# A four-layer network in one kernel: transposes widened to 128 columns, an MLP begun on one step's statistics, and a Fourier layer whose row 64 and last unit are rescheduled

## The chip, the cores and the metric

The kernel runs on one core of one Trainium2 chip, as one program. The metric is device time in microseconds (us), the median of three runs. The engines: PE multiplies matrices (PEld loads its weights), DVE works on vectors, ACT applies functions and copies, POOL is a second vector engine, SP issues the DMAs. On-chip memory is SBUF; matmuls write PSUM[...].

## The reference, cut to what matters

The input is x[4, 96, 64, 64]; with b = 4 images of L = 4096 tokens there are NT = 16384 tokens of C = 96 channels. Layer 0 (two Mamba blocks) and layer 2 (linear attention, a quantised MLP) are not touched by the change. Layer 1 and the first half of layer 3 are:

```python
# layer 1: depthwise 7x7 convolution, LayerNorm over channels, MLP with gelu, residual
h = conv7x7_depthwise(x, conv_w) + conv_b
h = transpose(h, (0, 2, 3, 1))
h = (h - mean(h)) * rsqrt(var(h) + eps) * ln_g + ln_b
h = gelu(einsum('bhwc,cf->bhwf', h, w1) + b1)          # 96 -> 384
x = transpose(einsum('bhwf,fc->bhwc', h, w2) + b2) * layer_scale + x
...
# layer 3, first half: Fourier mixing along the 4096 tokens, on t = LayerNorm(t)
h = relu(bn(einsum('bnc,hc->bnh', t, w1)))             # 96 -> 192
X = fft(h, axis=1)
xr = relu(X.real * rd - X.imag * idg + rb)
xi = relu(X.imag * rd + X.real * idg + ib)
y = ifft(xr + 1j * xi, axis=1).real
t = t + bn(einsum('bnh,ch->bnc', y, w2))
```

## The kernel before, in words

The residual stream `t` stays in SBUF as [96, 16384]. The layers follow each other; in the profiled execution layer 1 lies at about 2605 to 3011 us, the Fourier layer at 3300 to 3838 us, and the last quantised MLP behind it.

**Layer 1, turn.** `tokens` (L730) loads one of 16 chunks of 1024 tokens: layer 0's output `o` and the input `xr`, 393 KB each; ACT scales `o` and DVE adds the two (L737). `turn` (L739) brings the chunk to tokens on partitions: for each 128 tokens one matmul (L744) with the tokens as the weights (96 rows, 128 columns) and an identity of 96 columns as the moving operand. Four results share a PSUM tile; ACT copies the first four, DVE the second four (L748) into `xt`. A matmul on 32-bit data is two passes through PE, so a chunk has 16 passes. The next chunk's `tokens` is written ahead of each `turn`. Then the convolution follows as 24 groups of four channels, each four matmuls with 128x128 bands (L787, L790). `small` (L772) lends a slot of the same PSUM tag to `consts2`, which prepares weights of later layers at group 8.

**Layer 1, MLP.** The tokens come in 32 blocks of 512, in n = 8 steps k of four. `stats(k, d)` (L804) takes mean and variance of four rows of 128 tokens (bn_stats and bn_aggr on DVE); `roots(k)` (L813) makes rsqrt of a step's 16 variances on ACT, with Ln (L815) and Exp (L816), each behind a load of its table; `back(i)` (L818) normalises block i on DVE (L824), turns it back by four matmuls (L829) and copies it to `xc`; `hidden(i)` (L833) has three matmuls (L838) with gelu on ACT (L839); `out(i)` (L841) three matmuls (L844) and the addition to `t`. The order of each engine's instructions is written out by hand (L850 to L871): stats and roots of steps 0 and 1, then back(0) to back(3), then the steps. In step k, `hidden` of block 4k + d is followed by `back` of the block four ahead, stats of step k + 2, and `out` of the block before; roots(k + 2) ends the step.

**Fourier layer.** A transform over 4096 tokens is split into 128 x 32. There are eight units (image, half of the 192 hidden channels), and each unit has PER = 4 groups, so 32 groups `its`. The loop (from L1251) runs over j and is a software pipeline, again in an order written by hand. Iteration j has `over_n1(j)` (first transform, L1139), `fold(j-2)`, `over_n2(j-1)` (second, L1160 to L1163), and `over_k2(j-3)` (inverse over k2, L1208 and L1209, written to `bt`). Groups of unit u finish over_k2 in iteration 4u + 6. The real transform needs only 65 of 128 rows; row 64 takes a way of its own: `row64(u)` (L1215) multiplies (L1218), ACT copies to `r` (L1220), one DMA writes `r` to DRAM (`d<-r`, L1222) and a second one reads it back into row 64 of `bt` (`bt<-d`, L1223). It stands in iteration 4u + 7, behind over_k2. From iteration 4u + 8 on, unit u's eight blocks of four n follow, two in each iteration: `over_k1` (L1225) loads 256 KB of the inverse transform (`gt`), has four matmuls (L1230) into a `misc` bank, and ACT copies the result to `ys` (L1232); `w2` (L1234) multiplies it with the output weights (L1238) into another `misc` bank and DVE adds it to `t` (L1242 for half 0, L1244 for half 1). The order within an iteration with blocks is

```python
over_n1(j) ... fold(j - 2); over_k1(block 0); over_n2(j - 1) ...
w2(block 0); over_k1(block 1); over_k2(j - 3) ... row64; w2(block 1)
```

`misc` (L1098) has two PSUM banks, shared by six uses; tag `i1` of over_k2 has two as well. Iterations also carry work for the next image: LayerNorm (`norm1`, `norm2`) where unit j // 4 is even, `w1` ("tokens") where it is odd, and nothing for the last unit. Past j = 31 only the pipeline's rest is left; the last unit's blocks are iterations 36 to 39.

Of the kernel before, what the change touches and what calls it, by code (L numbers as in the profile page):

```python
# [9 lines left out]
F32 = mybir.dt.float32  # L10
# [8 lines left out]
B, C, HW, L = 4, 96, 64, 4096  # L19
# [31 lines left out]
class Net:  # L51
# [661 lines left out]
    def layer1(self, scratch, t):  # L713
# [4 lines left out]
        with ExitStack() as ctx:  # L718
# [4 lines left out]
            with (  # L723
                tc.manual_schedule(engines=engines),
                tc.tile_pool(name="l1a", bufs=1) as wk,
                tc.tile_pool(name="l1ap", bufs=1, space=PSUM) as psum,
            ):
                for at in (slice(0, 2), slice(NR + 2, NR + 4)):
                    nc.gpsimd.memset(xt[:, :, :, at], 0.0)
                def tokens(b, s):  # L730
                    at = slice(b * L + s * T, b * L + (s + 1) * T)
                    o = wk.tile([C, T], F32, name="o", tag="o", bufs=3)
                    nc.sync.dma_start(o, scratch[:, at])
                    xr = wk.tile([C, T], F32, name="xr", tag="xr", bufs=3)
                    nc.sync.dma_start(xr, ins["x"][b, :, s * T : (s + 1) * T])
                    nc.scalar.activation(o, o, AF.Identity, scale=self.osc, bias=self.osh)
                    nc.vector.tensor_add(t[:, at], o, xr)  # L737

                def turn(b, s):  # L739
                    for h in range(2):  # L740
                        ps = psum.tile([128, 4, C], F32, name="xt_ps", tag="xt", bufs=4)
                        for d in range(4):
                            a = b * L + s * T + (4 * h + d) * 128
                            nc.tensor.matmul(ps[:, d], t[:, a : a + 128], self.ident[:C, :C], start=True, stop=True)  # L744
                        r = 2 + s * (T // 128) + 4 * h
                        dst = xt[:, :, b, r : r + 4].rearrange("p c r -> p r c")
                        if h:
                            nc.vector.tensor_copy(dst, ps)  # L748
                        else:
                            nc.scalar.copy(dst, ps)  # L750

                chunks = [(b, s) for b in range(B) for s in range(NSC)]
                tokens(*chunks[0])
                for k, chunk in enumerate(chunks):
                    if k + 1 < len(chunks):
                        tokens(*chunks[k + 1])
                    turn(*chunk)

                def load(g):
                    w = wk.tile([128, GC, 4, 128], F32, name="band", tag="band", bufs=3)  # L760
                    nc.sync.dma_start(w, ins["band"][g])
                    return w

                def outer(g):

                    x2 = wk.tile([128, 2 * GC, B, NR], F32, name="x2", tag="x2", bufs=3)
                    at = slice(g * 2 * GC, (g + 1) * 2 * GC)
                    nc.gpsimd.tensor_copy(x2[:64], xt[:64, at, :, 4:])
                    nc.gpsimd.tensor_copy(x2[64:], xt[64:, at, :, :NR])
                    return x2  # L770

                def small(rows, cols):  # L772
                    ps = psum.tile([128, 4, C], F32, name="w_ps", tag="xt", bufs=4)
                    return ps.rearrange("p a c -> p (a c)")[:rows, :cols]

                x2 = [outer(0)]
                for g in range(C // GC):
                    if g == 8:
                        self.consts2(wk, small)
                    if g % 2 == 0 and g + 2 < C // GC:  # L780
                        x2.append(outer(g // 2 + 1))
                    w = load(g)
                    ps = psum.tile([128, GC, B, NR], F32, name="cv_ps", tag="cv", bufs=4)
                    for d in range(GC):
                        c = g * GC + d
                        for k, j in enumerate((1, 0, 2)):
                            nc.tensor.matmul(  # L787
                                ps[:, d], w[:, d, j], xt[:, c, :, 1 + j : 1 + j + NR], start=k == 0, stop=False
                            )
                        nc.tensor.matmul(ps[:, d], w[:, d, 3], x2[g // 2][:, g % 2 * GC + d], start=False, stop=True)  # L790
                    for d in range(GC):
                        c = g * GC + d
                        dst = xt[:, c, :, 2 : 2 + NR]
                        if g % 2:
                            nc.vector.tensor_scalar_add(dst, ps[:, d], cb[:, c : c + 1])
                        else:
                            nc.scalar.activation(dst, ps[:, d], AF.Identity, bias=cb[:, c : c + 1])
# [52 lines left out]
            n = NT // MB // 4  # L850
            with tc.manual_schedule(engines=engines):
                nc.scalar.preload_act_table_set(ACT_EXP_LN)
                for k in range(2):
                    for d in range(4):
                        stats(k, d)
                    roots(k)
                for d in range(4):
                    back(d)
                for k in range(n):
                    for d in range(4):  # L860
                        hidden(4 * k + d)
                        if k + 1 < n:
                            back(4 * k + 4 + d)
                        if k + 2 < n:
                            stats(k + 2, d)
                        if d:
                            out(4 * k + d - 1)
                    if k + 2 < n:
                        nc.scalar.preload_act_table_set(ACT_EXP_LN)
                        roots(k + 2)  # L870
                    out(4 * k + 3)  # L871
# [212 lines left out]
    def fourier(self, dram, t, h):  # L1084
        tc, nc, ins = self.tc, self.nc, self.ins
        CG, G, K1 = 24, 6, 65
        PER = CG // G
        units = [(b, half) for b in range(B) for half in range(2)]
        its = [(u, g) for u in range(len(units)) for g in range(0, CG, G)]
        with ExitStack() as ctx:  # L1090
# [7 lines left out]
            def misc(rows):  # L1098
                return pln.tile([128, MB], F32, name="m_ps", tag="m", bufs=2)[:rows]
# [98 lines left out]
            def over_k2(i):  # L1198

                u, g = its[i]  # L1200
                z = zz.pop(i)
                if g == 0:
                    bt[u] = wk.tile([N1, N2, C], F32, name="bt", tag="bt", bufs=2)
                for e in range(0, G, 3):
                    ps = pln.tile([N1, 3, 128], F32, name="i1_ps", tag="i1", bufs=2)
                    for d in range(3):
                        zd = z[:, e + d].rearrange("p k m -> p (k m)")
                        nc.tensor.matmul(ps[:, d], zd[:, 64:], bc, start=True, stop=False)  # L1208
                        nc.tensor.matmul(ps[:, d], zd[:, :128], bs, start=False, stop=True)  # L1209
                    nc.scalar.copy(  # L1210
                        bt[u].rearrange("p n (g c) -> p g n c", c=4)[:, g + e : g + e + 3],
                        ps.rearrange("p g (n c) -> p g n c", c=4),
                    )

            def row64(u):  # L1215
# [6 lines left out]
                nc.sync.dma_start(d.rearrange("o (n g c) -> g (o n) c", n=N2, c=4), r)  # L1222
                nc.sync.dma_start(bt[u][64:65].rearrange("p n c -> p (n c)"), d)  # L1223

            def over_k1(u, n, kept):  # L1225
                gt = wk.tile([N1, 4, N1], F32, name="gt", tag="gt", bufs=2)
                nc.sync.dma_start(gt, ins["idft"][:, n : n + 4])
                ps = misc(C).rearrange("p (n a) -> p n a", n=4)
                for d in range(4):
                    nc.tensor.matmul(ps[:, d], bt[u][:, n + d], gt[:, d], start=True, stop=True)  # L1230
                kept[u, n] = wk.tile([C, MB], F32, name="ys", tag="ys", bufs=2)
                nc.scalar.copy(kept[u, n], ps.rearrange("p n a -> p (n a)"))  # L1232

            def w2(u, n, kept):  # L1234

                b, half = units[u]
                ps = misc(C)
                nc.tensor.matmul(ps, self.a_w2[:, half, :], kept.pop((u, n)), start=True, stop=True)  # L1238
                ps = ps.rearrange("p (n a) -> p n a", n=4)
                td = ft[b][:, n : n + 4]  # L1240
# [6 lines left out]
            with tc.manual_schedule(engines=engines):  # L1247
                for n in range(0, N2, 2):
                    w1(0, n)
                kept, sq = {}, {}  # L1250
                for j in range(len(its) + 12):  # L1251
                    ub, k = divmod(j - 2 * PER, PER)
                    blocks = [(ub, n) for n in (8 * k, 8 * k + 4)] if 0 <= ub < len(units) else []

# [9 lines left out]

                    if j < len(its):
                        over_n1(j)

                    if normed:
                        norm1(b, a, sq)
# [18 lines left out]
                        over_k2(j - 3)  # L1288
                    if normed:
                        norm2(a, sq)  # L1290
                    if (j - 7) % PER == 0 and 0 <= (j - 7) // PER < len(units):
                        row64((j - 7) // PER)
                    turn(len(tokens))
                    if blocks:
                        w2(*blocks[1], kept)
                    if normed and k == PER - 1:
                        norm2(a + MB, sq)


def build(tc, ins, out):  # L1300
# [155 lines left out]
```

## Time and profile before

| | |
|---|---|
| runs | 3976.82, 3974.91, 3973.95 us; median 3974.91 |
| profiled execution | 3972.29 us; span in the trace 3970.5 us |
| mean granted PE clock | 0.858 of full |
| PE, DVE, ACT, POOL busy | 3291.6 (83%), 3155.9 (79%), 2419.9 (61%), 2912.9 (73%) us |
| gt<-in_idft | 64 DMAs of 256 KB |
| Fourier layer's iterations, start to start (L1139) | 11.6 to 15.4 us mostly; j = 12: 22.00, j = 20: 21.82, j = 28: 15.58 |

The busy share is an average over layers of which each has its own limit, so it says nothing of these stages. How to read what follows: a table by stretch of time gives each engine's busy time, the granted PE clock and the DMA share; the timeline lists instructions in order, with the idle time before them and its releaser in brackets; the waits list who waited for whom, with the sum, the number and the longest.

### The profile page before, as it was taken

To read this page: it belongs to the slowest core of one execution; us is meant where nothing else is said; L and a number is where in the kernel's file an instruction comes from. 1 tells how busy PE (TensorE), PEld (TensorE's weight loads), DVE (VectorE), ACT (ScalarE), POOL (GpSimd) and SP (SyncE) were. 2 spreads that over 40 slices of the span, in tenths; PEclk is the share of its full clock that TensorE was granted. 3 is DMA by queue.
4 is the path that set the end of the run, shared out by engine and by line. 5 is a ranking of instruction groups with operands and counts; after the bars stand their busy time and mean duration, and the time that the engine had idled before them with its cause. 6 is when DMAs were issued, how large, how long until landed. Compare 5 with 4: busy or idle time off the path is not lost. (4 is left out here: it accounts for less than half of the span.)

```text
span 3970.5 us, 45322 instructions
## 1 busy us (share of the span) xinstructions
PE 3291.6 (83%) x14174; PEld 1420.1 (36%) x14174; DVE 3155.9 (79%) x2772; ACT 2419.9 (61%) x4644; POOL 2912.9 (73%) x1443
## 2 busy tenths in 40 slices
PE   7888788888888778888878888677899998999878
PEld 3222222222222222222222222167445535666643
DVE  5999999999999999999999999941662384444539
ACT  4676667666666766677666666431345586655548
POOL 2999999999999999999999999911001064534417
PEclk8888888888887888788888888658899999999989
DMA  7567656756675667566666766566000000011111
GB/s 185 135 161 174 144 148 159 175 142 159 160 173 132 164 166 170 132 167 166 159 147 158 170 148 154 120 170 227 11 0 1 1 1 6 22 33 33 43 44 58
DMA packets 183291, 468.12 MB, mean 118 GB/s; under 512 B 53237, under 2 KB 55167, under 8 KB 179969
## 3 DMA queue, kind: packets, MB, share of 16 engines
q1 hardware_dynamic: 183048, 465.21, 47.1%
q8 instruction: 113, 1.85, 0.2%
q14 instruction: 130, 1.06, 0.1%
HBM read 391.53 MB, written 73.50 MB: 117 GB/s over the span
## 5 line engine op out<-in xcount | busy, mean ns | idle before, releaser
L496 POOL TENSOR_TENSOR hs<-hs,crep 128x1024 f32<-128x1024 f32 x768 | 1796.6, 2364 | 27.3 <-DVE hs L490 23.7
L454 PE MATMUL rep<-dbl,sel_b 32*128 32x512 f32 x1152 | 406.1, 781 | 464.1 <-DVE hs L490 433.4
L474 POOL TENSOR_TENSOR up<-udb,brep 128x1024 f32<-128x1024 f32 x256 | 605.1, 2364 | 8.5 <-DMA brep<-cd 8.5
L468 ACT ACTIVATE da<-ddb,nega 128x1024 f32<-128x1024 f32 x512 | 585.0, 1150 | 16.2 <-DVE hs L490 8.2
L468 ACT ACTIVATE dap<-ddb,nega 128x1024 f32<-128x1024 f32 x256 | 286.2, 1118 | 423.7 <-DVE hs L490 421.9
L515 PE MATMUL y<-hs,sel_r 128*32 128x512 f32 x3072 | 483.3, 689 | 6.5 <-POOL hs L496 6.4
L490 DVE TENSOR_TENSOR_SCAN hs<-da,state,rep 128x1024 f32<-128x1024 f32 x192 | 450.8, 2348 | 16.7
L490 DVE TENSOR_TENSOR_SCAN hs<-da,state,u 128x1024 f32<-128x1024 f32 x192 | 450.9, 2348 | 11.2 <-DVE u L486 1.4
L490 DVE TENSOR_TENSOR_SCAN hs<-dap,state,up 128x1024 f32<-128x1024 f32 x192 | 447.0, 2328 | 6.8 <-ACT dap L468 6.8
L454 PEld LDWEIGHTS rep<-dbl,sel_b 32*128 32x128 f32 x1152 | 109.0, 218 | 760.9 <-issue 512.8
L210 PE MATMUL ps<-n,w_x 97*64 97x512 f32 x1536 | 364.8, 617 | 9.4 <-ACT n L323 5.3
L486 DVE TENSOR_TENSOR u<-udb,rep 128x1024 f32<-128x1024 f32 x256 | 314.6, 1229 | 42.5 <-PE rep L454 11.3
L486 DVE TENSOR_TENSOR rep<-udb,rep 128x1024 f32<-128x1024 f32 x256 | 310.6, 1213 | 0.4
L1039 POOL CAST hq<-y 128x1536 fp8e5<-128x1536 f16 x64 | 93.9, 1467 | 253.7 <-issue 144.0
L210 PEld LDWEIGHTS ps<-n,w_x 97*64 97x64 f32 x1536 | 108.9, 140 | 257.5 <-issue 210.9
L515 PEld LDWEIGHTS y<-hs,sel_r 128*32 128x32 f32 x3072 | 66.9, 116 | 363.5 <-issue 195.8
L382 POOL TENSOR_TENSOR du<-delta,xc 128x512 f32<-128x512 f32 x96 | 122.6, 1277 | 67.4 <-ACT delta L366 52.2
L1178 POOL TENSOR_TENSOR av<-av,ec 128x780 f32<-128x780 f32 x32 | 58.8, 1837 | 150.1 <-ACT av L1175 150.1
L224 PE MATMUL ps<-xc,xproj 64*102 64x512 f32 x384 | 160.3, 998 | 3.5 <-ACT xc L344 3.5
L358 ACT COPY dbl<-ps 102x512 f32<-102x512 f32 x64 | 34.4, 589 | 207.1 <-PE ps L224 207.1
L911 POOL MEMSET h<- 1x4096 f32 x1 | 3.5, 3506 | 213.1 <-DVE n L824 213.1
L490 DVE TENSOR_TENSOR_SCAN hs<-da,rep 128x1024 f32<-128x1024 f32 x64 | 146.5, 2289 | 5.4
(256 smaller groups left out, 6492.9 us busy)
## 6 DMA issues: line engine op xcount, KB each, us to landing
ddb<-dd SPq DMA_DIRECT2D x768, 128.0 KB
udb<-ud SPq DMA_DIRECT2D x768, 128.0 KB
crep<-cd SPq DMA_DIRECT2D x512, 128.0 KB
brep<-cd SPq DMA_DIRECT2D x256, 128.0 KB
dd<-delta SPq DMA_DIRECT2D x64, 384.0 KB
ud<-du SPq DMA_DIRECT2D x192, 128.0 KB
band<-in_band SPq DMA_DIRECT2D x24, 1024.0 KB
gt<-in_idft SPq DMA_DIRECT2D x64, 256.0 KB
```

Of the source, the lines that this page charges most:

```text
L210: nc.tensor.matmul(ps[rows], w[:, 64 * p : 64 * p + 64], rhs[:, at.start + shift : at.stop + shift], start=k == 0, stop=k == len(ws) - 1, ...
L224: nc.tensor.matmul(ps, w[rows, p], x[rows, p], start=start and p == 0, stop=p == 2)
L382: nc.gpsimd.tensor_mul(u, m["delta"][:, of], m["xc"][:, of])
L454: nc.tensor.matmul(x[:, at], sel_b[rows, order[t][1]], made[k]["dbl"][rows, at], start=True, stop=True)
L468: nc.scalar.activation(da, made[k]["dd", h, j], AF.Exp, scale=nega[:, col : col + 1])
L474: nc.gpsimd.tensor_mul(u, made[k]["ud", h, j], made[k]["brep", g])
L486: nc.vector.tensor_mul(u, made[k]["ud", h, j], x)
L490: nc.vector.tensor_tensor_scan(hs[:, 1:], made[k].pop(("da", t)), u, 0.0 if s == 0 else st, ALU.mult, ALU.add)
L496: nc.gpsimd.tensor_mul(hs[:, :T], hs[:, 1:], made[k]["crep", order[t][1]])
L515: nc.tensor.matmul(made[k]["y", p][row : row + 32], sel_r, made[k]["hs", t][:, at], start=False, stop=True, skip_group_check=True,)
L1039: nc.gpsimd.tensor_copy(q, y2, saturate=False)
L1178: nc.gpsimd.tensor_add(v[:, 2:4], v[:, 0:2], ec)
```

## The change

In the turn, the matmul's moving operand has 128 columns (the identity's 96 rows, all its columns), and the PSUM tile is widened to 4 x 128[...]; the copies read the first 96 columns. In the MLP, only stats(0), roots(0) and back(0) stand ahead of the first hidden; back runs two blocks ahead instead of four; step 0 carries the stats of steps 1 and 2, and roots(1) stands behind hidden(2). In the Fourier layer row64(u) moves from iteration 4u + 7 to 4u + 6. The last unit's blocks leave the loop: all eight follow behind it, each over_k1 ahead of the w2 of the block before, and these w2 use the two `i1` banks. From j = 25 on, two loads of 1 MB into a free `hh` buffer take the place of the last 26 of the 256-KB loads.

```diff
-    ps = psum.tile([128, 4, C], F32, name="xt_ps", tag="xt", bufs=4)
+    ps = psum.tile([128, 4, 128], F32, name="xt_ps", tag="xt", bufs=4)
...
-    nc.tensor.matmul(ps[:, d], t[:, a : a + 128], self.ident[:C, :C], start=True, stop=True)
+    nc.tensor.matmul(ps[:, d], t[:, a : a + 128], self.ident[:C], start=True, stop=True)
...
-    nc.vector.tensor_copy(dst, ps)
+    nc.vector.tensor_copy(dst, ps[:, :, :C])
...
     nc.scalar.preload_act_table_set(ACT_EXP_LN)
-    for k in range(2):
-        for d in range(4):
-            stats(k, d)
-        roots(k)
     for d in range(4):
-        back(d)
+        stats(0, d)
+    roots(0)
+    back(0)
     for k in range(n):
         for d in range(4):
-            hidden(4 * k + d)
-            if k + 1 < n:
-                back(4 * k + 4 + d)
-            if k + 2 < n:
+            i = 4 * k + d
+            hidden(i)
+            if k == 0 and d == 2:
+                nc.scalar.preload_act_table_set(ACT_EXP_LN)
+                roots(1)
+            for i2 in (1, 2) if i == 0 else (i + 2,):
+                if i2 < 4 * n:
+                    back(i2)
+            if k == 0:
+                for d2 in (2 * (d % 2), 2 * (d % 2) + 1):
+                    stats(1 + d // 2, d2)
+            elif k + 2 < n:
                 stats(k + 2, d)
             if d:
-                out(4 * k + d - 1)
+                out(i - 1)
...
+    def fetch(k):
+        g = wk.tile([N1, CG, N2, 4], F32, name="hh", tag="hh", bufs=3)
+        g = g.rearrange("p g n c -> p (g n c)")[:, : N2 // 2 * N1].rearrange("p (n a) -> p n a", n=N2 // 2)
+        nc.sync.dma_start(g, ins["idft"][:, k * N2 // 2 : (k + 1) * N2 // 2])
+        for n in range(0, N2 // 2, 4):
+            late[k * N2 // 2 + n] = g[:, n : n + 4]
...
     def over_k1(u, n, kept):
-        gt = wk.tile([N1, 4, N1], F32, name="gt", tag="gt", bufs=2)
-        nc.sync.dma_start(gt, ins["idft"][:, n : n + 4])
+        if n in late:
+            gt = late[n]
+        else:
+            gt = wk.tile([N1, 4, N1], F32, name="gt", tag="gt", bufs=2)
+            nc.sync.dma_start(gt, ins["idft"][:, n : n + 4])
...
     def w2(u, n, kept):
-        ps = misc(C)
+        if u < len(units) - 1:
+            ps = misc(C)
+        else:
+            ps = pln.tile([N1, 4, 128], F32, name="i1_ps", tag="i1", bufs=2)[:C].rearrange("p n a -> p (n a)")
...
-    for j in range(len(its) + 12):
+    for j in range(len(its) + 4):
...
+        if j in (len(its) - 7, len(its) - 3):
+            fetch((j - len(its) + 7) // 4)
...
-        if (j - 7) % PER == 0 and 0 <= (j - 7) // PER < len(units):
-            row64((j - 7) // PER)
+        if (j - 6) % PER == 0 and 0 <= (j - 6) // PER < len(units):
+            row64((j - 6) // PER)
...
+    last = [(len(units) - 1, n) for n in range(0, N2, 4)]
+    for k, block in enumerate(last):
+        over_k1(*block, kept)
+        if k:
+            w2(*last[k - 1], kept)
+    w2(*last[-1], kept)
```

More of the change, by code (lines that the diff above doesn't have):

```diff
@@ L747, in turn @@
                         if h:
-                            nc.vector.tensor_copy(dst, ps)
+                            nc.vector.tensor_copy(dst, ps[:, :, :C])
                         else:
-                            nc.scalar.copy(dst, ps)
+                            nc.scalar.copy(dst, ps[:, :, :C])
                 chunks = [(b, s) for b in range(B) for s in range(NSC)]
@@ L772, in small @@
                 def small(rows, cols):
-                    ps = psum.tile([128, 4, C], F32, name="w_ps", tag="xt", bufs=4)
+                    ps = psum.tile([128, 4, 128], F32, name="w_ps", tag="xt", bufs=4)
                     return ps.rearrange("p a c -> p (a c)")[:rows, :cols]
@@ L1204, in over_k2 @@
                 for e in range(0, G, 3):
-                    ps = pln.tile([N1, 3, 128], F32, name="i1_ps", tag="i1", bufs=2)
+                    ps = pln.tile([N1, 4, 128], F32, name="i1_ps", tag="i1", bufs=2)[:, :3]
                     for d in range(3):
@@ L1223, in row64 @@
                 nc.sync.dma_start(bt[u][64:65].rearrange("p n c -> p (n c)"), d)
-            def over_k1(u, n, kept):
-                gt = wk.tile([N1, 4, N1], F32, name="gt", tag="gt", bufs=2)
-                nc.sync.dma_start(gt, ins["idft"][:, n : n + 4])
+            late = {}
+            def fetch(k):
[4 more added lines that the diff above has]
+                    late[k * N2 // 2 + n] = g[:, n : n + 4]
+            def over_k1(u, n, kept):
+                if n in late:
[3 more added lines that the diff above has]
+                    nc.sync.dma_start(gt, ins["idft"][:, n : n + 4])
                 ps = misc(C).rearrange("p (n a) -> p n a", n=4)
```

## Prediction

> **What bounds the kernel now.** No engine alone: PE is busy 83% of the span, but the change touches four stretches, each with its own limit. I read first the busy time by stretch, because it gives the granted clock (PEclk) of each. Columns: stretch, length, busy time of PE, weight loads, DVE, ACT, POOL, clock, DMA share, GB/s.
>
> ```profile
> 2614.00:2669.00 55.00, 54.42 (x255) 54.42 (x256) 28.66 (x31) 28.91 (x31) 0.00 (x0) 0.50 0.95 262
> 2676.00:2690.00 14.00, 14.00 (x128) 14.00 (x127) 2.26 (x8) 2.29 (x8) 4.78 (x5) 1.00 0.76 253
> 2842.00:3011.00 169.00, 167.14 (x529) 79.73 (x527) 95.45 (x309) 74.48 (x105) 4.06 (x2) 1.00 0.00 1
> 3765.00:3838.00 73.00, 50.27 (x247) 34.38 (x246) 22.90 (x26) 19.98 (x42) 5.73 (x4) 0.84 0.18 51
> ```
>
> Row 1 is layer 1's turn: PE is never idle, at half clock. Row 2, the convolution's 128-column passes, runs at full clock: 14.00/128 = 0.109 us a pass, against 54.42/255 = 0.213 in the turn. Row 3, the MLP's steady part, is PE-bound at full clock, 24.66 us a step. Row 4 is the Fourier tail, PE busy 69%.
>
> Next the timeline, for the pace inside the turn (start, length, engine, line, in brackets idle time before and its releaser):
>
> ```profile
> 2616.35 1.22 DVE L737 TENSOR_TENSOR t<-o,xr 96x1024 f32<-96x1024 f32 x1 [1.83 <-DMA xr<-in_x]
> 2619.42 1.22 DVE L737 TENSOR_TENSOR t<-o,xr 96x1024 f32<-96x1024 f32 x1 [0.27 <-DMA xr<-in_x]
> 2629.24 1.20 DVE L737 TENSOR_TENSOR t<-o,xr 96x1024 f32<-96x1024 f32 x1
> 2632.66 1.20 DVE L737 TENSOR_TENSOR t<-o,xr 96x1024 f32<-96x1024 f32 x1
> ```
>
> The first chunks come every 3.07 us, as the loads land; later ones every 3.41, which is 16 passes of 0.213. PE sets the pace by only 0.34 us a chunk.
>
> The MLP's start, PE and ACT:
>
> ```profile
> 2800.61 0.22 ACT L816 ACTIVATE rs<-rs 128x16 f32<-128x16 f32 x1
> ...
> 2814.01 1.99 PE L829 MATMUL tp_ps<-ident,n 128*96 128x128 f32 x8 [1.14 <-DVE n L824]
> 2815.79 4.45 PE L838 MATMUL g_ps<-xc,c_w 96*128 96x512 f32 x6
> ```
>
> Roots(0) is done 15 us before the first hidden; in between PE waits for DVE, block by block, and is cold (six L838 in 4.45 us; 2.74 later).
>
> Last the waits in the Fourier layer and the timeline around them:
>
> ```profile
> PE m_ps L1238 <- ACT ys L1232: 23.3, 23, 4.5
> PE m_ps L1230 <- DMA bt<-d: 13.9, 5, 4.9
> PE m_ps L1230 <- issue: 7.9, 2, 4.7
> ```
>
> ```profile
> 3679.43 1.50 PE L1139 MATMUL s_ps<-dft,hh 128*128 128x130 f32 x12
> 3685.66 1.10 PE L1238 MATMUL m_ps<-ys,a_w2s 96*96 96x512 f32 x2 [1.23 <-ACT ys L1232]
> ```
>
> ```profile
> 3472.47 0.33 SPq L1222 DMA_DIRECT2D d<-r  x1
> 3475.41 0.24 SPq L1223 DMA_DIRECT2D bt<-d  x1
> 3477.94 1.94 PE L1230 MATMUL m_ps<-gt,bt 128*96 128x128 f32 x8 [2.95 <-DMA bt<-d]
> 3770.96 1.99 PE L1230 MATMUL m_ps<-gt,bt 128*96 128x128 f32 x8 [4.89 <-DMA bt<-d]
> 3812.57 1.99 PE L1230 MATMUL m_ps<-gt,bt 128*96 128x128 f32 x8 [4.73 <-issue]
> 3830.54 1.10 PE L1238 MATMUL m_ps<-ys,a_w2s 96*96 96x512 f32 x2 [0.73 <-ACT ys L1232]
> 3831.48 1.04 PE L1230 MATMUL m_ps<-gt,bt 128*96 128x128 f32 x8
> ```
>
> The first pair is an undisturbed iteration: 6.23 us from L1139 to L1238. In the others each unit's first L1230 waits for row 64's two DMAs in series; the "issue" rows of that length stand at the same place. After the wait eight passes take 1.94 to 1.99 us, not 1.04: the clock has fallen too. In the tail each block waits 0.73 us for ACT's copy.
>
> **What the Trainium skill says.** "TensorE: Matmul & The Clock Gate", "Part 1: The HAM clock gate": half rate is the default, full rate follows a busy window of about 3.4 us, an idle one drops it. The doubled L1230 agrees; the turn does not, 55 us without a gap at 0.50. There 96 columns stream in a pass paced by 128, so 75% of the time; I infer that this is too thin, because the convolution (128 of 128) gets full clock. "LDWEIGHTS" in the same page: load time goes by the weights' columns, P/1.2 ns, 107 for 128; the trace's 0.109 agrees, and 0.213 for 96 moving columns shows that the load sets the pitch. "ScalarE: Activation LUTs", "What ACT_TABLE_LOAD costs": 1.28 us a load plus a drain; the trace shows 1.28 and no separate drain. "DMA: Bandwidth & Descriptors", "Anatomy of one DMA — SWDGE (gpsimd) path", gives about 2.0 us fixed for DMAs that GpSimd issues; this pair, issued by SP, took 2.93 and 2.39 in the chain of waits.
>
> **The change part by part.** Sums stand against the profiled execution, 3972.29 us (span 3970.5, 1.8 around it); the runs' median is 2.6 above it.
>
> *Turn, L744.* Still 256 passes, each streaming 128 columns. At half clock the pitch stays 0.213, as the convolution's first, cold passes show (six in 1.27): no cost. If the clock is released, a chunk needs 16 × 0.109 = 1.74 us of PE and the DMAs decide: 786 KB at 262 GB/s = 3.0. I take 3.03 a chunk: the last L737 starts at 2613.30 + 15 × 3.03 = 2658.8 instead of 2663.37, and its last copy ends about 4.0 later (1.2 addition, 1.7 passes, copy) at 2662.8 instead of 2670.35. Gain 7.5 (0 if not released, 10 if the loads come faster). Copies read the same 96 columns: nothing. The convolution starts sooner by as much, and its wait for loads at group 8 moves along, because the loads are queued behind the turn's; 0.3 more for small().
>
> *MLP start.* Removed ahead of the first hidden (2815.79): 16 stats at 0.42 us = 6.7, roots(1), and three back at 3.1 us. n(0) now waits for roots(0), whose last result is at 2800.83, so hidden(0) starts at about 2804.3, 11.5 earlier. But step 0 then carries on DVE 32 stats (13.4 us) and six back, and PE waits for these: for back(2), then after each eight stats. back(4) needs roots(1), on ACT behind block 2's gelus and a 1.28 us load; PE idles about 3.6 us there, enough to drop the clock (about 3.4 lost). Laid out queue by queue, step 1's hidden begins at 2842.4 (2839.0 if the clock holds) against 2842.17, with six instead of eight back done: 2 × 0.875 = 1.75 us of PE work (L829, 1.04 a row with overlap) left for later. Net 1.3 slower taken, from 1.5 faster to 2 slower.
>
> *Row 64 one slot ahead.* The chain is PE 0.62, ACT 0.24, DMAs 2.9 to 3.6 and 1.9 to 2.5: 6.5 us. It gets a whole iteration of 11.6 to 15 us. Its matmul, copy and two DMAs only change iteration; on SP the pair moves behind one gt load and ahead of the next. What is late next: PE reaches L1230 at once, then L1238 waits for ACT's ys, which stands behind the fold. Where no wait exists, L1238 starts 6.23 us after the iteration's L1139, as shown (6.22 from 3730.46); with tokens I estimate 6.3. Units 1, 3, 5 have 9.68, 11.07, 10.28 now: gains 3.4, 4.7, 4.0. Units 2 and 4 wait 0.83 and 1.66, mostly taken over by ys: 0.2 and 0.4. Unit 0 waits for nothing: 0. Unit 6: the wait 4.89 and a cold start, 5.1 together; the ys wait of 4.46 at 3787.26 remains. Sum 17.8.
>
> *Last unit.* From w2's end, 3807.84, to the next stage's first matmul, 3838.14: 30.3 us, made of the 4.73 wait, two blocks at half clock, and a pitch of 2.70 a block (3828.78 to 3831.48). With another over_k1 ahead of each w2, ACT's copy (0.58) hides beside 0.89 us of PE: 8 × (0.89 + 0.86) = 14.0, then 1.2 for DVE's last addition. Gain 15.1. Four banks give each producer two buffers; DVE's 1.2 a block is below 1.75. The two idft loads of 1 MB replace 26 of 256 KB. fetch(1) stands ahead of unit 5's bt<-d and about 4 us later it lands; I estimate 4.6 us of margin left. If the cover is gone, 4 us. Fourier: 33.3, range 27 to 38.
>
> *Next stage.* Its first 15 us run at a clock of 0.56, 4.4 us a block against about 3.1 later. After a dense tail PE enters warm, but streams only about half the time. Between 0 and 4 × 1.3 = 5; I take 2.
>
> Sum: -7.5 - 0.3 + 1.3 - 33.3 - 2.0 = -41.8. On the median: 3933. About 0.2% (8 us) is what a measurement here can tell from no change.
>
> **Rivals.**
> - *The turn's clock is not released*: 3940.5. For: plain multiplication by an identity has not been seen at full clock here. Against: same pass shape as the convolution.
> - *Another wait takes row 64's place*: ys, PSUM or gt late in units 1 to 6, half of 17.8 and a bit more lost: 3943. For: ACT's ys wait is already the largest PE wait (23.3 us). Against: iterations without a bt wait run at 11.58.
> - *More than forecast*: the next stage fully warm and no clock drop in the MLP: 3927.
> - *It doesn't do what it says*: row 64 still late behind the SP queue and the tail still serial: about 3970, no change.
> - *Slower*: the turn's loads no longer overlap its matmuls: 2 × 0.213 a pass, 256 × 0.213 = 54.5, instead of -7.5: 3995. It decides from a pass pitch of 0.213 + 34.3/256 = 0.35 us. Against: the convolution's equal passes at 0.213 cold.
>
> **How the numbers follow.** Forecast 0.60 (own range 3925 to 3941), clock 0.14, other wait 0.14, more 0.06, no effect 0.03, slower 0.03. The range 3920 to 3948 holds the first four with the ends of the unknown costs (the Fourier layer at 27 or 38, the next stage at 0 or 5), and leaves out little more than the last two. Faster 0.94, same 0.03, slower 0.03.
>
> **What would show it.** Turn: clock 1.00 after about 3.4 us and L737 every 3.0; at 0.50 the clock rival is right. MLP: first L838 near 2804 minus the turn's gain, a gap of 3 to 4 us ahead of back(4), step 1 no earlier than before. Fourier: no wait for bt<-d ahead of L1230, and L1238 about 6.3 after L1139 in all units; tail pitch 1.75. The prediction is wrong if ys or gt is waited for where bt was, or if the turn stays cold.

## The result and the profile after

The changed kernel takes 3931.34 us (median of four runs, 3925.47 to 3932.20) against 3974.43 (four runs, 3963.18 to 3976.82) for the kernel before: a ratio of 0.9894, 95% interval 0.9873 to 0.9915. The forecast was 3933. The profiled execution, 3925.47, is the fastest of the four; its span is 3923.7, 46.8 less than before. The same landmarks in both traces cut the span into stages. Two of them are the moment at which DVE begins to wait for an instruction, not the instruction itself: the first addition starts 4.02 us behind its landmark before and 3.53 after, the first stats 1.08 in both.

| stage, from landmark to landmark | before | after | moved | forecast |
|---|---|---|---|---|
| up to DVE's wait for the first addition L737 | 2609.28 | 2607.41 | -1.87 | 0 |
| turn, to the end of its last copy | 61.06 | 52.31 | -8.75 | -7.5 |
| convolution, to DVE's wait for the first stats | 119.30 | 117.36 | -1.94 | -0.3 |
| MLP, to layer 2's first center product | 221.58 | 221.57 | 0.0 | +1.3 |
| layer 2, to the first over_n1 | 306.85 | 300.50 | -6.35 | 0 |
| Fourier layer, to its last w2 | 518.97 | 490.82 | -28.15 | -33.3 |
| last MLP, to the end | 133.47 | 133.72 | +0.25 | -2.0 |

The busy time by stretch of the changed kernel (columns as before): the turn, the MLP's end into layer 2, unit 7's iterations, the last unit's blocks, the start of the last MLP.

```profile
2612.00:2659.00 47.00, 35.70 (x256) 33.03 (x256) 29.49 (x32) 30.38 (x31) 0.00 (x0) 0.92 1.03 281
2998.00:3015.00 17.00, 13.29 (x51) 6.34 (x52) 3.35 (x5) 9.62 (x17) 6.84 (x2) 1.00 0.00 0
3692.00:3739.00 47.00, 42.09 (x261) 31.83 (x260) 30.74 (x36) 27.07 (x74) 24.45 (x17) 1.00 0.01 2
3775.00:3790.00 15.00, 14.55 (x81) 9.38 (x79) 9.01 (x8) 5.81 (x9) 0.00 (x0) 1.00 0.01 1
3791.00:3806.00 15.00, 12.61 (x17) 3.53 (x18) 1.57 (x3) 6.46 (x11) 0.00 (x0) 0.59 0.00 1
```

PE is called warm below when it runs at full clock, and cold at half. The turn's clock is 0.92 and the DMAs are busy all the time; the last unit keeps PE busy 14.55 of 15 us; but the last MLP starts as cold as before (0.59). The second row is the surprise. The same stretch of the kernel before reads

```profile
3011.00:3028.00 17.00, 14.67 (x24) 5.41 (x25) 2.23 (x4) 6.79 (x11) 6.41 (x2) 0.58 0.00 0
```

so layer 2's first blocks, in which no line was changed, ran at full clock after and at half before. The timeline of the changed kernel at the places that the prediction named (turn, block 4 of the MLP, unit 1, last unit):

```profile
2636.22 2.05 PE L744 MATMUL xt_ps<-ident,t 96*128 96x128 f32 x16 [1.09 <-DVE t L737]
...
2791.58 5.46 PE L838 MATMUL g_ps<-xc,c_w 96*128 96x512 f32 x6 [0.78 <-DVE xc L831]
...
2814.22 1.99 PE L829 MATMUL tp_ps<-ident,n 128*96 128x128 f32 x8 [3.13 <-DVE n L824]
...
3457.74 1.04 PE L1250 MATMUL m_ps<-gt,bt 128*96 128x128 f32 x8
...
3464.46 1.10 PE L1261 MATMUL m_ps<-ys,a_w2s 96*96 96x512 f32 x2 [3.07 <-ACT ys L1252]
...
3783.65 1.04 PE L1250 MATMUL m_ps<-hh,bt 128*96 128x128 f32 x8
3784.52 1.02 PE L1261 MATMUL i_ps<-ys,a_w2s 96*96 96x512 f32 x2
3785.39 1.04 PE L1250 MATMUL m_ps<-hh,bt 128*96 128x128 f32 x8
```

A chunk's 16 passes take 2.05 us and then wait for the addition, that is for the loads. The waits for bt<-d ahead of over_k1 (now L1250) are gone in every unit (none is left among the trace's waits); in unit 1 w2 (now L1261) waits 3.07 us for ACT's ys instead. The last unit's pitch is 1.74 us.

### The profile page after: what moved, and what is told of

Read it like the earlier page. It is cut to its first block, busy times and chain, and to the rows that moved or that the text cites. A ratio compares the mean times of both kernels' runs of the same rounds, so it can differ in the third digit from the quotient of the medians.

```text
span 3923.7 us, 45255 instructions
## 1 busy us (share of the span) xinstructions
PE 3245.2 (83%) x14174; PEld 1384.0 (35%) x14174; DVE 3158.5 (80%) x2772; ACT 2419.1 (62%) x4644; POOL 2911.1 (74%) x1443
```

## The experiments

Stages below are the table's. All times of a kernel stand beside runs of the kernel before on the same chip; in brackets are the ratio and its 95% interval. A difference from the changed kernel's 3931.34 is one between chips, on which the kernel before had medians of 3972.46 to 3974.43.

**e1: the turn alone.** The kernel before with the diff's lines of `turn` and `small`.

> The kernel before with the 128-column turn alone (tile, moving operand, copies, small). Theory: the streaming share decides the clock; the turn runs at clock 1.00 after its first windows, 16 passes take 2.05 us or less, the last turn copy stands 8 to 9 us after-like earlier relative to the first addition (52.3 us from first addition to last copy instead of 61.1), the convolution starts warm (about 2 us more), and the whole is 10.5 us faster: about 3964 against 3974.5. Rival 1: the turn gained from loads that happened to come earlier, then the clock would be 0.50 here in some part and the gain 2 to 4. Rival 2, on the 6.3 us that layer 2 was faster by in the changed kernel's trace: if that was where the clock's window happened to fall, layer 2 may be warm or cold here (3011 to 3318: 306.9 us cold, 300.5 warm); if the MLP's new order caused it, it is cold here, 306.9.

Measured: 3962.65 against 3972.46, ratio 0.9974 (0.9966 to 0.9982). Turn 51.69 us at clock 0.96 (2612 to 2659), convolution 118.10: 10.6 less in the two. Layer 2: 306.86, cold. The clock explains the turn, and in this trace a warm turn didn't bring a warm layer 2.

**e5 and e10: how full must a pass be?** As e1, with 112 and with 120 moving columns:

```diff
-  nc.tensor.matmul(ps[:, d], t[:, a : a + 128], self.ident[:C], ...)
+  nc.tensor.matmul(ps[:, d, :112], t[:, a : a + 128], self.ident[:C, :112], ...)   # e5; e10: 120
```

> The kernel before with a turn of 112 moving columns (87.5% of a pass), PSUM tile as in the 128-column turn. Theory (streaming share decides): between 75%, which never released the clock in 55 us, and 100%, which released it in the second window; if the bound lies below 87.5%, the turn takes 52 us as with 128 columns, 10 us faster in all; if above, 61 us at 0.50, no change. Rival (anything but the share, for instance the padded tile or whole-bank writes, did it): like 128 columns whatever the count. The trace's clock in the turn tells; a released clock does not refute the theory, a clock at 0.50 refutes the rival.

> The kernel before with a turn of 120 moving columns (94% of a pass). Theory: the share of a window in which PE streams decides, with a bound between 88% (112 columns, never released) and 100% (128, released): 120 columns tell on which side 94% lies; the convolution's first windows stream 94% and are followed by full clock, so I expect a release and a turn as with 128 columns (52 to 59 us, as the loads come), 5 to 10 us faster. Rival (whole 128-column results are needed, not a share): clock 0.50 for the whole turn, 61 us, no change.

Measured: 3972.20 against 3973.09 (1.0002, 0.9993 to 1.0010) and 3972.50 against 3973.15 (0.9993, 0.9984 to 1.0001); turns of 60.74 and 61.35 us. The prediction's first stretch, the turn, in e5 and then in e10:

```profile
2614.00:2669.00 55.00, 54.23 (x254) 54.23 (x255) 29.10 (x31) 29.31 (x31) 0.00 (x0) 0.50 1.00 267
```

```profile
2614.00:2669.00 55.00, 54.62 (x254) 54.34 (x255) 28.55 (x31) 28.90 (x31) 0.00 (x0) 0.50 0.95 263
```

Neither 88% nor 94% releases the clock; 128 of 128 columns did, behind one or two steps of 3.41 us of the clock's record (the trace's list of when the granted clock changed). My guess for 120 was wrong, and with it the reason that I gave. The share of the time in which PE streams columns is not the rule: in the tail of the kernel before, the clock was released behind cold blocks that each wait for ACT:

```profile
3815.29 2.02 PE L1238 MATMUL m_ps<-ys,a_w2s 96*96 96x512 f32 x2 [0.73 <-ACT ys L1232]
3817.10 1.91 PE L1230 MATMUL m_ps<-gt,bt 128*96 128x128 f32 x8
3819.74 1.10 PE L1238 MATMUL m_ps<-ys,a_w2s 96*96 96x512 f32 x2 [0.73 <-ACT ys L1232]
```

With 128 columns in 0.213 us and 512 in four times that, I estimate that PE streams there for 69% and 81% of the last two steps at half clock; behind them it is at full clock (1.10), while 94% in the turn never was. What sets the turns of 96, 112 and 120 columns apart is that each pass streams fewer columns than its weights have, and all three keep the same pitch of 0.213, so that each pass waits for the next weights; with 128 none does. That this is the reason is inferred; it wasn't tried with other data or other weights, and e10's rival, that whole results of 128 columns are needed, fits the same runs. The padded tile is ruled out, since e5 and e10 have it.

**e2 and e11: the MLP's start alone, and everything but it.** The kernel before with the diff's lines from `n = NT // MB // 4` on; the changed kernel without them.

> The kernel before with the MLP's new start alone. Theory: the first hidden comes 11.6 us earlier, step 1's hidden 1.75 us earlier, and at the MLP's end nothing is left (0.0 in the changed kernel's trace, because two blocks of back are still owed); so no change within 1 us, unless layer 2's start is warm by it: then 6 us faster, in the trace at the first blocks behind the MLP. Rival: the order causes the warm start of layer 2 (every trace with this order has it, and none without). The forecast's own value was 1.3 slower.

> The changed kernel with the MLP's old start. Theory: the MLP's new start is worth 0.0 to 0.5 us (what it gains before step 1 is owed in blocks of back), so 3931 to 3932, unless the phase of the clock's window at layer 2's start changes with it (then 6 slower). Rival: the new start is worth the 3.7 us that it showed alone in the times; then 3935.

Measured: e2 3968.81 against 3972.46 (0.9990, 0.9981 to 0.9998); e11 3937.68 (0.9911, 0.9897 to 0.9924), 6.3 more than the changed kernel, though the intervals of the two overlap. The MLP stage takes 221.10 in e2 and 221.83 in e11, against 221.58 in the kernel before and 221.57 in the changed one: at most 0.5 by itself. The 3.65 by which e2's times are shorter are more than its trace shows, whose layer 2 is cold (306.95); a warm layer 2 in some of its other executions would explain them, but isn't shown. What e11's trace loses is layer 2: 306.83 us, cold.

```profile
3004.00:3021.00 17.00, 14.61 (x25) 5.46 (x26) 2.29 (x4) 6.78 (x11) 6.46 (x2) 0.59 0.00 0
```

Over all eleven traces whose layer 2 has no surplus work, it lasts 306.7 to 307.0 us in eight (before, e1 to e5, e10, e11) and 300.4 to 300.5 in three (after, e6, e7), nothing between. The clock's record tells them apart. It changes only at the edges of steps of 3.41 us, and layer 2's first center product starts 0.39, 0.49 and 0.58 us behind such an edge in after, e7 and e6, but 0.60 in e2 and 0.63 to 1.2 in the old order's traces (worked out from the records). The clock at the MLP's start changes on an edge, and from there the MLP is PE-bound, so its end nearly keeps its place in the step: in these traces the new order shifts that place by some tenths, past a point near 0.59. (It isn't fixed: in e9, which has the new order and surplus work in layer 2, it is 2.36.) The point is drawn after the fact, between two traces 0.02 us apart, and no run moved a start across it on purpose; that the place in the step is the cause, and why, is inferred, not shown. But both my theories were too simple: free chance would not sort the traces so, and it isn't the order's own doing, since e2 has the order and was cold.

**e12 and e8: warm starts made certain.** One surplus matmul, not part of the reference and never read, behind each of the first five center products of layer 2 and of the last MLP, in the kernel before (e12) and in the changed one (e8):

```diff
+  def fill(count):
+      ps = psum.tile([C, MB], F32, name="o_ps", tag="o")      # last MLP: tag "y"
+      for _ in range(count):
+          nc.tensor.matmul(ps, self.center, t[:, 8 * MB : 9 * MB], start=True, stop=True)
...
   center(j)
+  if j < 5: fill(1)
```

> The kernel before with the surplus matmuls alone, five at layer 2's start and five at the last MLP's (added work that the reference doesn't have). Theory: the 6.3 us by which layer 2 was shorter in the changed kernel's trace are a warm PE at its first blocks, nothing of the change itself: here, where every trace without it was cold, the surplus makes it warm, 301.5 us from center to Fourier instead of 306.9, and 129.7 instead of 133.5 at the end: 9 us faster, 3964. Rival: the surplus costs what it saves, no change.

> The changed kernel with one surplus matmul (center times a block of t, into a bank not yet in use, never read) behind each of the first five center products of layer 2 and of the last quantised MLP. The added work is outside the reference. Theory: whether these two stages start warm is chance of where the clock's window falls on a PE that streams some 60% of the time; with the surplus it streams 85% and stays warm every time: layer 2 takes 300.5 us from its first center to the Fourier layer's first product, the last MLP about 4 us less than the 132 of the changed kernel's trace; the median falls by 6 to 10 against the changed kernel, about 3923, and the runs spread less. Rival: the surplus is in the way (0.86 us each, 10 in all), then slower by up to 8.

Measured: e12 3962.24 against 3973.15 (0.9968, 0.9956 to 0.9981). Both stretches of e12 at clock 1.00:

```profile
3013.00:3030.00 17.00, 16.10 (x55) 7.29 (x56) 3.19 (x5) 8.73 (x15) 6.68 (x2) 1.00 0.00 1
3833.00:3848.00 15.00, 13.64 (x33) 4.79 (x34) 3.93 (x7) 9.03 (x16) 0.93 (x1) 1.00 0.01 2
```

Layer 2 takes 301.29, the last MLP 129.56: 9.5 less in the two, with no line of the change in it. Layer 2's first center product stands 0.68 behind an edge there, where the traces without surplus were cold. So the 6.35 us are a warm PE. e8: 3928.72 (0.9894, 0.9877 to 0.9911), 2.6 below the changed kernel by its median and level by the ratio, where I expected 6 to 10. Its trace has the last MLP at 129.71, 4.0 less, and layer 2 at 301.52, 1.0 more than the changed kernel's, which was warm already. The times alone don't settle 2.6 us.

**e3 and e4: row 64 alone, the tail alone.** The kernel before with `(j - 7)` made `(j - 6)`; the kernel before with the last unit's loop, the `i1` banks and `fetch`.

> The kernel before with row 64 one iteration earlier, nothing else. Theory: no wait for bt<-d before any unit's first product of over_k1; units 1 and 3 end at 8.06 us from over_n1 to w2 (gains 1.6 and 3.0, as the iteration before still has a norm2 on ACT and POOL), unit 5 gains 4.0, unit 6 about 5.3, unit 7 4.8 (wait) and up to 1.8 (clock), unit 0 loses 1.7: sum 19 us faster, 3955. Rival: the 1.7 loss at unit 0 is chance of the clock window, then 0 there, and 21 in sum. Rival from the forecast (another wait takes its place): half, 10.

> The kernel before with the last unit's blocks pipelined over four banks and the two loads of 1 MB, row 64 left where it was. Theory: the pitch of the last unit's blocks falls from 2.70 to 1.74 us, so 7 x 0.96 = 6.7 us, and up to 1.5 from less time at half clock; the wait for bt<-d of 4.7 ahead of the last unit stays. Sum 7 to 8 us faster, 3967. Rival: the large loads delay row 64's pair of units 5 and 7 (queued on SP ahead of it), 2 to 4 us of the gain lost there.

Measured: e3 3955.05 against 3972.46 (0.9961, 0.9949 to 0.9974); e4 3958.59 (0.9967, 0.9956 to 0.9979): 17.4 and 13.9 less. In the traces the Fourier layer gains 12.98 in e3 and 8.86 in e4, 21.8 in sum, and 28.15 with both. (e3's traced execution took 3959.59, 4.5 more than its median.) Most of what e3's trace lacks against its 19 is in unit 7. Its first product still waits for row 64, and the serial blocks behind it run cold for three steps of the clock, two in the kernel before:

```profile
3798.40 1.48 PE L1230 MATMUL m_ps<-gt,bt 128*96 128x128 f32 x8 [0.89 <-DMA bt<-d]
3800.60 2.02 PE L1238 MATMUL m_ps<-ys,a_w2s 96*96 96x512 f32 x2 [0.73 <-ACT ys L1232]
...
3806.87 1.92 PE L1230 MATMUL m_ps<-gt,bt 128*96 128x128 f32 x8
3809.51 1.10 PE L1238 MATMUL m_ps<-ys,a_w2s 96*96 96x512 f32 x2 [0.73 <-ACT ys L1232]
```

With both edits there is no wait at that place and the tail is dense from its first block. From unit 6's last w2 to the last w2 of all it takes 29.20 us before, 26.60 in e3, 20.74 in e4 and 14.66 with both, so there the edits give 3.5 more together than in sum. The other 2.8 of the 6.3 are in places that also differ between traces that have both edits: unit 6's blocks take 35.87 us in the changed kernel, 37.13 in e7, and iteration 20 takes 18.45 and 20.08. The times show no such surplus: the four edits of e1 to e4 alone sum to 44.7, the whole change gives 43.1. e4's unit 7 gains 8.6 from its first product on, a little over the 7 to 8 expected, and in its trace the last MLP starts warm (129.42, 4 less); I did not foresee that, and no large load was in the way. In e3 unit 0 loses 1.71 us as in the changed kernel.

**e7: row 64 behind the w1 blocks.** In the changed kernel unit 0's row 64 competes with w1 for the two misc banks:

```profile
3376.73 0.62 PE L1225 MATMUL m_ps<-dft,z 128*24 128x128 f32 x4
3377.28 1.20 PE L1132 MATMUL m_ps<-a_w,h 97*128 97x192 f32 x4
3379.77 1.35 PE L1132 MATMUL m_ps<-a_w,h 97*128 97x192 f32 x4 [1.29 <-ACT r L1227]
3380.91 2.81 PE L1146 MATMUL s_ps<-dft,hh 128*128 128x130 f32 x12
```

PE waits for ACT to empty row 64's bank, and over_n1 behind it is cold (2.81 instead of 1.50). e7 writes `turn(len(tokens))` ahead of `row64`.

> The changed kernel with row 64 behind the iteration's remaining w1 blocks instead of ahead of them. Theory: at unit 0 row 64 takes one of the two misc banks while the w1 blocks need both, and PE waits for ACT's copy (1.29 us in the trace) and then runs cold; behind them nothing waits, and the 1.7 us that unit 0 lost come back: iterations 6 and 7 take 24.8 together instead of 26.5. Rival: the loss is the clock's window by chance, then it may be there or not. Under 0.1%, so the trace decides, not the times.

Measured: 3932.84 (0.9906, 0.9891 to 0.9921); iterations 6 and 7 take 26.53 us in sum, as in the changed kernel. My theory of the place fell; in e7's trace row 64 itself waits:

```profile
3382.00 1.98 PE L1132 MATMUL m_ps<-a_w,h 97*128 97x192 f32 x8
3385.51 0.70 PE L1225 MATMUL m_ps<-dft,z 128*24 128x128 f32 x4 [1.54 <-ACT hh L1134]
3386.14 2.97 PE L1146 MATMUL s_ps<-dft,hh 128*128 128x130 f32 x12
```

Three users of two banks (PSUM buffers), emptied late by ACT: the order only chooses who waits; e9 below shows it.

**e6: ys ahead on ACT.** The changed kernel, with fold's last step (the negation) issued behind over_k1.

```diff
-  fold(j - 2)
+  neg = fold(j - 2)          # returns the nc.scalar.mul instead of issuing it
   if blocks: over_k1(*blocks[0], kept)
+  neg()
```

> The changed kernel with ACT's last step of fold (the negation of zz) put behind over_k1's copy ys on ACT. Theory: what is late in the Fourier iterations now is ACT's copy, because it stands behind that negation, which waits for DVE; w2 of the first block then starts as soon as over_n2 is through, about 5.0 us after over_n1's start instead of 6.2 (8.06 after a norm2), and iterations of 11.58 become about 10.3: 1.2 in some 23 iterations plus 3 in units 1 and 3, up to 29 us faster than the changed kernel, 3902. Rival: the chain through POOL and ACT (av) takes its place at once, then under 10 us, 3925.

Measured: 3917.95 (0.9865, 0.9848 to 0.9881), 13.4 below the changed kernel; Fourier layer 476.75, 14.1 less. The waits of PE for ys, of the changed kernel and then of e6:

```profile
PE m_ps L1261 <- ACT ys L1252: 29.4, 23, 4.0
```

```profile
PE m_ps L1261 <- ACT ys L1252: 7.5, 11, 2.8
```

Of 21.9 us of waits that are gone 14.1 become time. Iterations of 11.58 and 14.66 us come down by 0.9, those with a LayerNorm by 0.1. The result lies between theory and rival: ys was the limit in about half the iterations.

**e9: three edits.** The changed kernel with e6's and e8's edits, and row 64's product in a bank of tag `xi` in place of `misc`.

> The changed kernel with three edits: ys ahead of the negation (worth 13.4 by the run before), the surplus matmuls at the start of layer 2 and of the last MLP (added work that the reference doesn't have), and row 64's product in the xi bank instead of a misc bank. Theory: the last MLP starts warm (129.7 us from the last w2 to the end, not 133.7), unit 0 loses nothing to row 64 (iterations 6 and 7 take 24.8 together), and the whole is 3931 - 13.4 - 4.0 - 1.7 = 3912. Rival for row 64: the bank was not what PE waited for and the clock falls anyway, then 26.5 again and 3914.

Measured: 3906.41 against 3973.15 (0.9833, 0.9819 to 0.9846), the best of all and 25 below the changed kernel. Iterations 6 and 7 take 23.47 us, where e6 and e8, which have the other two edits, take 26.52 and 26.51, so the bank was what PE waited for; the Fourier layer takes 470.56, the last MLP 129.63.

## Why the prediction was right, and where not

- **Total.** Right in size, and in part by luck: two errors cancel in the trace, since the Fourier layer gave 5.1 less than forecast, and layer 2 gave 6.35 that no step had. e11, whose trace has a cold layer 2, took 3937.68, still in the range 3920 to 3948. The trace is the fastest of four executions, 5.6 to 6.7 below the others; whether layer 2 was warm in those is not known. And a sum was off: 17.8 and 15.1 make 32.9 for the Fourier layer, not 33.3. It took 490.82, 493.31 and 490.89 us in the three traces that have its part of the change and no other edit there (after, e8, e11), 25.7 to 28.2 less than before.
- **Turn.** The step is right: clock released, DMAs then decide (e1, e5, e10). The 7.5 was priced from the first addition itself to the last copy, which took 57.04 us before and 48.78 after, 8.3 less. It could have come out smaller: with the clock released the table's turn takes 51.7 to 58.7 us in seven traces, against 60.3 to 61.9 in the seven without, because the loads' pace now shows; e6's, the slowest, moved 248 GB/s where the changed kernel's moved 281. The kernel before hid that behind PE. The rival of a cold turn was weaker than I made it: a multiplication by an identity does run at full clock in the kernel before, L829 in the MLP, eight passes in 1.04 us at clock 1.00. The reason that I inferred, "75% is too thin", is wrong as a share: 94% was as cold, and the tail was released behind a step of about 81%. That 128 columns match the weights was enough for the forecast.
- **Convolution.** It starts warm behind a warm turn: 117.4 to 119.2 us in the seven traces with 128 columns, against 119.3 to 121.5 in the others. I had taken 0.3, for small() only.
- **MLP.** Right in mechanism: first hidden 11.65 earlier against the stats, a 3.13 us wait at block 4 that drops the clock, and the two owed blocks eat the rest: step 1's hidden was 1.75 earlier, the end 0.0. I had 1.3 slower.
- **Layer 2.** No step looked at it. In eleven traces it stayed warm or fell cold as its start stood in the clock's step (e11 above); the reason is inferred.
- **Row 64.** The waits are gone. Units 5 and 6 gave 9.05 together (forecast 9.1), unit 4 0.42 (0.4). Units 1 and 3 gave 1.79 and 3.37, not 3.4 and 4.7: "with tokens I estimate 6.3" failed. (Unit 3's is one trace's: with row 64 moved, iteration 20 takes 18.45 to 20.36 us in seven traces.) After an iteration with a norm2 it is 8.05 to 8.07 from over_n1 to w2, since ACT's negation waits for DVE (3.42 us in unit 1) and ys stands behind it; with ys ahead of the negation, in e6, it is 4.84. Unit 0 was put at zero and lost 1.71: three users of two misc banks (e7, e9).
- **Last unit.** 15.55 with unit 6's end, against 15.1; pitch 1.74. The DMA margin of fetch(1) held.
- **Last MLP.** 2.0 taken, none came: cold in the changed kernel's trace, warm in e4's. The range 0 to 5 was right, but no trace shows a middle value: the stage takes 133.5 to 133.8 us or 129.4 to 129.7, and 134.9 in e5 and e10.
- **Rivals.** "Another wait takes row 64's place" was partly true, for units 1 and 3; PE's waits for ys went from 23.3 to 29.4 us. The slower one, passes that no longer overlap, is ruled out by 2.05 us for 16 passes.

## What to carry to other kernels

When a wait is removed, time the next arrival from the same kind of iteration, with its neighbours' leftovers on the in-order engines, and count the users of every buffer in the slot that the step moves to. Where a stage leaves PE half idle, price its start twice, warm and cold, and not at the mean; a few surplus matmuls kept it warm in all three traces that had them. An edit that shortens one engine's work can expose the spread of another's, as with the turn's loads.

## What the runs showed of the hardware

- PE without a recorded pause stayed at half clock for 55 us at 112 and at 120 of 128 columns a pass; at 128 the clock was released behind one or two full steps of 3.41 us, in seven traces. The Trainium skill ("TensorE: Matmul & The Clock Gate", "Part 1: The HAM clock gate") says that a busy window of about 3.4 us releases it; here windows that the profile shows as busy throughout were not enough, and the page doesn't say what counts as busy.
- Once released, the changed kernel's turn kept full clock for 40 us with 16 to 20 passes in a step (27 in the first), where some 31 of 0.109 us would fit. e8's fell to half for two steps, behind a step with 15.
- The start of layer 2 costs 6.3 us more or not, that of the last MLP about 4.1 (e4's 129.42 against 133.47 before); the eight cold traces of layer 2 agree to 0.3 us, the three warm ones to 0.1. Much of the spread of single runs (3967.41 to 3979.54 in 27 runs of the kernel before) is as large as such steps; that they cause it was not tried.
